# Zero matmuls in TensorE's planned gaps at the start of a two-layer cross-attention and feed-forward kernel

## The chip, the cores and the metric

The kernel runs on one core of a Trainium2 chip. The metric is the device time of one execution in microseconds (us); several runs are summed up by their median. The profile belongs to one profiled execution, and its span reaches from the first to the last instruction on the core.

## The reference, cut to what matters

The input is `x`, 8192 tokens of width 128 in 128 sequences of 64 tokens, and a context of the same shape. Four blocks are added onto `x` one after the other, in float32:

```
x = x + xattn0(layernorm(x), ctx)   # 16 heads of width 8, softmax over 64 keys, gate, layer norms
x = x + ffn0(layernorm(x))          # silu(x w1) * (x w2), gelu(. h1), gelu(. h2), . w3 ; hidden 512
x = x + xattn1(layernorm(x), ctx)   # 16 heads, softmax over 64 keys
x = x + ffn1(layernorm(x))          # relu(x W1 + b1) W2 + b2 ; hidden 512
```

## The kernel before

**Tiling.** The 8192 tokens are cut into 16 chunks of 512 tokens (`NCH`, `CH`). A chunk lies in SBUF as 4 groups of 128 tokens. For each chunk there are four streams of work, which are Python generators: `attention0`, `ffn0`, `attention1` and `ffn1`. Attention handles a chunk in two halves of four sequences (`attend`). The steps of one half are: "scores" on TensorE (line 519), the row maximum on VectorE (line 523), four small VectorE steps that split the maximum into three bf16 parts (532 to 535), "max transpose" on TensorE (538), its copy on ScalarE (541), "scores less max" on TensorE (550), the exponential on ScalarE (555), "weighted values" on TensorE (569), two masked copies on ScalarE (579, 580), the sums and the reciprocal on VectorE (582 to 587), and the product on GpSimd (598). The output projection is "tokens" (`token_major`, line 623). `normalised` holds a layer norm (394 to 421), `transposed` the four transposes (431) and their copy (436 or 438), and `queries`, `keys` and `values` the projections (447, 460, 475). The feed-forward block `ffn0` has "w12" (724, 725), its tanh and products (728 to 732), and the two 512 by 512 layers "h" (764).

**Order.** The program's order on every engine is fixed while the program is being built, by a planner, the class `Order`. Each stream yields `Op`s, one for each stage on one engine. `LENGTHS` gives each name its planned duration and a lag, both in planned us. The planner keeps a clock for each engine. It repeatedly takes the operation that can start earliest in planned time, with priorities between the streams, advances that engine's clock, and lets the generator emit its instructions. An operation on one engine can start after an operation on another by the constant `LAT` (0.08) and that operation's lag. Buffers are planned too: `RESOURCES` counts the slots of each kind, among them the eight PSUM banks ("bank"; scores use banks 0 to 3 together), and a released slot carries the planned time from which it is free. What the chip does is not bound to those times: there each engine runs its own instructions in the planned order, and waits only for data and buffers.

**The start.** Loads are issued from SyncE in the order written in the code. GpSimd first makes constants (the identity, `vblk` of line 328, `nmax` of line 337), and then helps with the layer norms (382, 383). The first TensorE operation is a bias matmul in `constants` (643); after it come the transposes and projections of chunks 0 and 1, then their attention halves (chunk 0, then chunk 1), and then chunk 0's `ffn0`. The streams of chunk 2 wait until the first large layer of chunk 0's `ffn0` is under way (`AHEAD`, `marks`).

**The context for the second attention** is loaded turned (line 291), token by token into columns, into slots of kind "c".

Of the kernel before, what the change touches and what calls it, by code (L numbers as in the profile page):

```python
# [9 lines left out]
BF16 = mybir.dt.bfloat16  # L10
# [4 lines left out]
P = 128  # L15
# [33 lines left out]
}  # L49
TRACE = []  # L50
AHEAD = 2
SWAP = [*range(16, 32), *range(16)]

LAT = 0.08
PE, DVE, ACT, POOL, SP = "PE", "DVE", "ACT", "POOL", "SP"
# [22 lines left out]
class Op:  # L78
# [5 lines left out]
    def __init__(self, engine, name, get=None, put=(), after=None, table=None, prio=None):  # L84
        self.engine, self.name, self.get, self.put = engine, name, get or {}, list(put)
        self.after, self.table, self.prio, self.end = after, table, prio, None
        self.us, self.lag = LENGTHS[name]
# [14 lines left out]
class Order:  # L102
# [4 lines left out]
    def __init__(self, resources):  # L107
        self.clock = dict.fromkeys((PE, DVE, ACT, POOL, SP), 0.0)
        self.free = {k: [(0.0, i) for i in range(n)] for k, n in resources.items()}
        self.table, self.streams, self.waiting, self.log = None, [], [], []  # L110
        self.tiling = 0

    def add(self, gen, prio, deps=()):
# [19 lines left out]
    def choice(self, kind, n, t):  # L133


        if kind == "sc":
            f = [x for x in self.free["bank"] if x[1] < 4]
            return f if len(f) == 4 else None
        f = self.free[kind]
        if kind == "bank":  # L140
            f = sorted(f, key=lambda x: (max(x[0], t), x[1] < 4, x[0]))
        else:
            f = sorted(f)
        return f[:n] if len(f) >= n else None

    def advance(self, s, value=None):
        while True:
            try:
                got = s.gen.send(value)
            except StopIteration:  # L150
                s.done = True
                if s in self.streams:
                    self.streams.remove(s)
                return
            if isinstance(got, tuple):
                value = Stream(got[0], got[1], ())
                value.ends = list(s.ends)
                self.streams.append(value)
                self.advance(value)
            elif isinstance(got, list):  # L160
                s.op, s.deps = None, got
                return
            else:
                s.op = got
                return
# [15 lines left out]
    def run(self):  # L181
        while True:
            self.begin()
            best = None
            for n, s in enumerate(self.streams):
                if s.op is not None:
                    t = self.start_of(s)
                    if t is not None:
                        other = s.op.table not in (None, self.table)
                        prio = s.prio if s.op.prio is None else s.op.prio  # L190
                        key = (t + (0.6 if other else 0.0), prio, n)
                        if best is None or key < best[0]:
                            best = (key, s, t)
            if best is None:
                assert not self.streams and not self.waiting
                return
            _, s, t = best
            op, op.slots = s.op, {}
            for kind, n in op.get.items():
                f = self.choice(kind, n, t)  # L200
                kind_of = "bank" if kind == "sc" else kind
                op.slots[kind] = [(kind_of, i) for _, i in f]
                self.free[kind_of] = [x for x in self.free[kind_of] if x not in f]
            op.end = t + op.us
            if op.engine == PE and TILING.get(op.name, 0) != self.tiling:
                self.tiling = TILING.get(op.name, 0)
                op.end += CHANGE
            if op.table not in (None, self.table):
                self.table = op.table
                op.end += 1.3  # L210
            self.clock[op.engine] = op.end
            for kind, i in op.put:
                self.free[kind].append((op.end + LAT + max(op.lag, 0.0), i))
            self.log.append((op, [op.after] if op.after else s.ends, t))
            s.ends = [op]
            self.advance(s, op)
# [3 lines left out]
def kernel(  # L220
# [16 lines left out]
    nc = tc.nc  # L237
# [4 lines left out]
    const = ctx.enter_context(tc.tile_pool(name="const", bufs=1))  # L242
# [6 lines left out]
    banks = psum.tile([P, 8, DH], F32, tag="banks", name="banks")  # L249
# [23 lines left out]
    def load(name, shape, src):  # L273
        t = const.tile(shape, F32, tag=name, name=name)
        nc.sync.dma_start(t, src)
        return t
# [17 lines left out]
    order = Order(RESOURCES)  # L294
# [12 lines left out]
    wf1 = load("wf1", [P, DH], w_f1)  # L307
    wf2 = load("wf2", [P, 4, D], w_f2)

    ident = const.tile([P, P], F32, tag="ident", name="ident")  # L310
    make_identity(nc, ident)

# [13 lines left out]
    for i in range(N_VB):  # L326
        t = resident.tile([P, 32, 3, 2, 8], F32, tag=f"vblk{i}", name=f"vblk{i}")
# [7 lines left out]
    for i in range(N_NM):  # L335
        t = resident.tile([P, 4, 32], BF16, tag=f"nmax{i}", name=f"nmax{i}")
# [167 lines left out]
    def attend(got, half):  # L504
# [61 lines left out]
        for s in range(HS):  # L566
# [20 lines left out]
        nc.vector.stream_shuffle(  # L587
            rec.rearrange("p s q -> p (s q)"), su.rearrange("p s q -> p (s q)"), SWAP
        )
# [101 lines left out]
    def attention0(ci, prio):  # L691
        got = {"free": []}
        xt = x_sb[ci]
        con = yield (context0(ci, got, prio), prio)
        z, fz = yield from normalised(xt, twice=True)
        if ci == 0:
            consts.append((yield (constants(), prio)))
        yield consts
        gat = yield (gate0(z, got), prio)
        qnT, fq = yield from transposed(z, (), colv("L0_xattn_ln_q_g"), colv("L0_xattn_ln_q_b"))  # L700
        got["qx"], f = yield from queries(wa0[:, 0, :], qnT, bq0, fq)
        got["free"] += f
        yield [con, gat]
        yield Op(DVE, "free", put=fz)
        if ci == 0:
            biases[0] = yield from out_bias(wa0[:, 3, :], "L0_xattn_bv", "L0_xattn_bo", "bo0")
        oT, fo = yield from attention(got, prio)
        po, fp = yield from token_major([(oT, wa0[:, 3, :])], fo)
        op = yield Op(DVE, "from bank", get={"wk": 1}, put=fp)
        o = tile_of(op.slots["wk"][0], (P, NG, D))  # L710
        nc.vector.tensor_tensor(o, po, biases[0], ALU.add)
        y, fy = yield from normalised(o, gate=got["gate"])
        yield Op(POOL, "add 3", put=fy + op.slots["wk"])
        nc.gpsimd.tensor_tensor(y, y, rowv("L0_xattn_ln_o_g"), ALU.mult)
        nc.gpsimd.tensor_tensor(xt, xt, rowv("L0_xattn_ln_o_b"), ALU.add)
        nc.gpsimd.tensor_tensor(xt, xt, y, ALU.add)  # L716
# [127 lines left out]
    for ci in range(NCH):  # L844
        marks.append(Stream(None, 0, ()))
        a0.append(order.add(attention0(ci, 1), 1, a0[-2:-1] + marks[-AHEAD - 1 : -AHEAD]))
        first = ci == NCH - 1
# [56 lines left out]
```

## Time and profile before

| | |
|---|---|
| median of 3 runs | 1228.09 us (1226.3 to 1228.68) |
| time of the profiled execution | 1228.58 us |
| its span | 1226.8 us |
| mean granted TensorE clock over the span | 0.976 |
| busy: PE, PEld | 1158.8 us (94%), 708.0 us (58%) |
| busy: DVE, ACT, POOL | 891.3 us (73%), 578.2 us (47%), 329.9 us (27%) |
| chain that ended last: PE, DVE, ACT | 78%, 16%, 2% |
| PE busy from 14.28 to 96.44 us | 55.09 of 82.16 us, at a mean granted clock of 0.69 |
| PE busy from 96.44 us to the end | 1103.70 of 1130.36 us |

PE is TensorE's matmul side, PEld its weight load, DVE VectorE, ACT ScalarE, POOL GpSimd, SP SyncE. PEclk is the clock that TensorE was granted, as a share of full speed. The chain that ended last is followed back from the last instruction; "issue" in it is time in which nothing that the profile shows was waited for. A line such as `L569` is line 569 of the kernel, `x64` the number of instructions merged, and a float32 matmul of one call shows as two instructions.

### The profile page before, as it was taken

The page shows a single profiled execution, that of the slowest core. Times are in us where ns is not written, and L with a number is a line of the kernel's source. Part 1 is how long each engine was busy: PE and PEld are TensorE (multiplying, and loading weights), DVE is VectorE, ACT ScalarE, POOL GpSimd, SP SyncE. Part 2 cuts the span into 40 slices and gives each one's busy share as a digit, 9 for nine tenths or more (in the row PEclk, how much of TensorE's full clock was granted, in tenths as well). Part 3 has the DMA queues.
Part 4 walks back from the last instruction along what each step waited for, and adds up shares of the span by engine and source line. Part 5 has one row for each costly group of instructions (what it writes and reads, how often), then busy time and mean ns, then how long its engine had stood idle before and what let it go on. Part 6 is the DMA issues. An engine that isn't in the chain of part 4 may idle for free.

```text
span 1226.8 us, 31151 instructions
## 1 busy us (share of the span) xinstructions
PE 1158.8 (94%) x13446; PEld 708.0 (58%) x13446; DVE 891.3 (73%) x2357; ACT 578.2 (47%) x733; POOL 329.9 (27%) x505
## 2 busy tenths in 40 slices
PE   4669999999999999999999999999999999999998
PEld 2544555565655656565655557565565556546676
DVE  5565677697769877777768869766897768822795
ACT  2124555644456454445556374445636564333310
POOL 5041142133214241413214313221423113401310
PEclk9569999999999999999999999999999999999999
DMA  9999994919197990949397891999993000000001
GB/s 213 10 23 24 25 10 20 16 13 9 19 8 30 7 31 2 8 29 9 20 8 22 14 24 11 9 6 16 9 9 11 2 2 2 10 1 1 10 19 43
DMA packets 1075753, 23.11 MB, mean 19 GB/s; under 512 B 1050016, under 2 KB 1074592, under 8 KB 1075488
## 3 DMA queue, kind: packets, MB, share of 16 engines
q1 hardware_dynamic: 1075616, 21.13, 87.4%
q8 instruction: 105, 1.72, 0.8%
q14 instruction: 32, 0.26, 0.1%
HBM read 16.93 MB, written 4.19 MB: 17 GB/s over the span
## 4 chain that ended last, share of the span: by engine, by line
PE 78%; DVE 16%; ACT 2%; issue 1%; POOL 1%; DMA 1%; SPq 0%; DVEq 0%; ACTq 0%
PE banks L764 32%; PE banks L623 10%; PE banks L550 7%; PE banks L569 5%; PE banks L519 4%; PE banks L724 4%; PE banks L810 4%; PE banks L725 4%; DVE m L523 3%; PE banks L475 2%; DVE wk L421 2%; PE banks L431 2%; PE banks L447 2%; PE banks L460 2%; DVE st L394 2%
## 5 line engine op out<-in xcount | busy, mean ns | idle before, releaser
L764 PE MATMUL banks<-hid,wh 128*128 128x512 f32 x1024 | 475.8, 602 | 1.5 <-DVE hid L732 1.3
L764 PEld LDWEIGHTS banks<-hid,wh 128*128 128x128 f32 x1024 | 183.3, 190 | 187.9 <-issue 167.2
L523 DVE TENSOR_REDUCE m<-banks 128x32 f32<-128x2048 f32 x64 | 146.2, 2284 | 30.9 <-PE banks L519 30.7
L598 POOL TENSOR_TENSOR wk<-av,rec 128x256 f32<-128x256 f32 x64 | 46.7, 730 | 452.1 <-DVE rec L587 384.0
L738 ACT ACTIVATE hid<-banks,col 128x512 f32<-128x512 f32 x128 | 87.9, 687 | 167.8 <-PE banks L764 167.3
L555 ACT ACTIVATE e<-banks 128x2048 f32<-128x2048 f32 x64 | 120.1, 1877 | 25.0 <-PE banks L550 24.5
L586 DVE RECIPROCAL su<-su 128x256 f32<-128x256 f32 x64 | 111.5, 1743 | 0.1
L582 DVE SCALAR_TENSOR_TENSOR su<-banks,mask,su 128x256 f32<-128x256 f32 x64 | 30.9, 482 | 103.4 <-ACT av L580 102.8
L383 POOL TENSOR_TENSOR nr<-nv,neg_half 128x4 f32<-128x4 f32 x96 | 97.5, 1015 | 8.0
L738 ACT ACT_TABLE_LOAD x62 | 79.5, 1283 | 29.5 <-PE banks L764 28.6
L519 PEld LDWEIGHTS banks<-kx,qx 32*128 32x128 f32 x2048 | 65.8, 193 | 42.5 <-issue 13.7
L541 ACT COPY nmT<-banks 128x128 bf16<-128x128 bf16 x64 | 16.9, 264 | 154.6 <-PE banks L538 147.8
L569 PEld LDWEIGHTS banks<-e,vblk 128*32 128x32 f32 x4096 | 62.9, 113 | 43.6 <-ACT e L555 29.8
L569 PE MATMUL banks<-e,vblk 128*32 128x64 f32 x4096 | 73.8, 225 | 9.7 <-ACT e L555 7.9
L519 PE MATMUL banks<-kx,qx 32*128 32x128 f32 x2048 | 78.5, 290 | 3.0 <-DVE m L523 2.6
L728 ACT ACTIVATE wk<-banks,half_s 128x512 f32<-128x512 f32 x64 | 43.9, 687 | 74.0 <-PE banks L724 73.2
L550 PE MATMUL banks<-qx,kx 32*128 32x128 f32 x2048 | 75.5, 286 | 0.8 <-issue 0.8
L724 PE MATMUL banks<-wk,w 128*128 128x512 f32 x128 | 68.5, 618 | 2.7 <-DVE wk L438 2.7
L555 ACT ACT_TABLE_LOAD x48 | 61.6, 1283 | 13.9 <-PE banks L550 12.6
L550 PEld LDWEIGHTS banks<-qx,kx 32*128 32x128 f32 x2048 | 66.2, 196 | 1.7 <-issue 1.7
L394 DVE BATCH_NORM_STATS2 st<-x 128x6 f32<-128x128 f32 x256 | 55.3, 278 | 16.0 <-POOL x L716 11.5
L725 PE MATMUL banks<-wk,w 128*128 128x512 f32 x128 | 66.5, 601 | 0.0
(113 smaller groups left out, 1738.7 us busy)
## 6 DMA issues: line engine op xcount, KB each, us to landing
c<-in_c_dram SPq DMA_DIRECT2D x32, 256.0 KB, 41.1
x<-in_x_dram SPq DMA_DIRECT2D x16, 256.0 KB, 3.5
out_dram<-x SPq DMA_DIRECT2D x16, 256.0 KB, 2.3
wh<-in_w_h_dram SPq DMA_DIRECT2D x1, 2048.0 KB, 11.5
wa<-in_w_a_dram SPq DMA_DIRECT2D x2, 256.0 KB, 5.9
w<-in_w_dram SPq DMA_DIRECT2D x1, 512.0 KB, 7.1
wf<-in_w_f_dram SPq DMA_DIRECT2D x2, 256.0 KB, 7.2
row<-in_rows_dram SPq DMA_DIRECT2D x1, 384.0 KB, 5.4
```

Of the source, the lines that this page charges most:

```text
L383: nc.gpsimd.tensor_tensor(rs, ve, neg_half, ALU.pow)
L519: nc.tensor.matmul(sc[:, g, s, :], qs[h, s, :], ks[h, s, :], start=True, stop=True)
L523: nc.vector.tensor_reduce(m, sc.rearrange("p g s (j k) -> p g (s j) k", j=2), AX.X, ALU.max, negate=True,)
L550: nc.tensor.matmul(sT[:, g, s, :], lhs, rhs, start=(n == 0), stop=(n == 1), skip_group_check=True)
L555: nc.scalar.activation(e.rearrange("p g s i q -> p (g s i q)"), sT.rearrange("p g s c -> p (g s c)"), AF.Exp, scale=SCALE,)
L569: nc.tensor.matmul(po[32 * g : 32 * g + 32, i, s, :], vb[:, 4 * (half * HS + s) + g, i : i + 2].rearrange("p h j d -> p (h j d)"), e[:, g, ...
L586: nc.vector.reciprocal(su, su)
L623: nc.tensor.matmul(ps[:, g, :], lhs[:, g * P : (g + 1) * P], w, start=(n == 0), stop=(n == len(blocks) - 1),)
L724: nc.tensor.matmul(pa, w12[:, 0, k * P : (k + 1) * P], zT, start=True, stop=True)
L725: nc.tensor.matmul(pb, w12[:, 1, k * P : (k + 1) * P], zT, start=True, stop=True)
L738: nc.scalar.activation(h, ps, AF.Gelu, scale=scale)
L764: nc.tensor.matmul(ps, wh[:, l, k, o * P : (o + 1) * P], hid[k][0], start=(k == 0), stop=(k == 3))
```

## The change

A bf16 tile `blank` of 128 by 128 is set to zero by GpSimd, ahead of the identity and all other constants. A function `busy(n, bank)` issues `n` matmuls of `blank` with `blank`, each 128 by 128 by 128, into the first 128 columns of a PSUM bank; nobody reads them. Sixty of them go into bank 7 before anything else on TensorE. Beyond that, whenever the planner places a TensorE operation whose planned start is below 95 (`RAMP`), it first calls `fill`: the planned gap before that operation, times 0.8, divided by 0.11 (`FILLER`) and cut to a whole number, is the number of zero matmuls that are issued ahead of it, into the free bank with the highest number that the operation itself does not take. The planner's clocks and slots are not changed by this, so the order of all other work stays what it was.

```
+RAMP, FILLER = 95.0, 0.11
...
         self.table, self.streams, self.waiting, self.log = None, [], [], []
+        self.busy = None
...
+    def fill(self, t, op):
+
+        n = int((t - self.clock[PE]) * 0.8 / FILLER)
+        taken = [i for f in op.slots.values() for kind, i in f if kind == "bank"]
+        free = [x for x in self.free["bank"] if x[1] not in taken and x[0] <= self.clock[PE] + 0.2]
+        if n > 0 and free:
+            self.busy(n, max(free, key=lambda x: x[1])[1])
...
                 self.free[kind_of] = [x for x in self.free[kind_of] if x not in f]
+            if op.engine == PE and t < RAMP:
+                self.fill(t, op)
             op.end = t + op.us
...
     wf2 = load("wf2", [P, 4, D], w_f2)
 
+    blank = const.tile([P, P], BF16, tag="blank", name="blank")
+    nc.gpsimd.memset(blank, 0.0)
+
+    def busy(n, bank):
+        for _ in range(n):
+            nc.tensor.matmul(banks[:, bank, 0:P], blank, blank, start=True, stop=True)
+
+    order.busy = busy
+    busy(60, 7)
     ident = const.tile([P, P], F32, tag="ident", name="ident")
```

## The prediction

> **What bounds the kernel now.** I read the page's 40 slices first. From slice 3 on PE is busy 90% or more and so it is TensorE that sets the time; before that it is not busy, and its clock is not full either.
>
> ```profile
> PE   4669999999999999999999999999999999999998
> PEclk9569999999999999999999999999999999999999
> ```
>
> So slices 0 to 2, some 92 us, are a stage of their own. I then cut it into stretches of 3.41 us, because the points at which the granted clock changes (27.55, 30.96, 34.38, 71.92, 78.75, 88.99 us) all lie on one such grid. The columns are the stretch, its length, busy us of PE, PEld, DVE, ACT and POOL, granted clock, DMA share and GB/s.
>
> ```profile
> 24.14:27.55 3.41, 1.16 (x4) 0.40 (x6) 0.11 (x2) 2.57 (x6) 0.00 (x0) 1.00 1.88 7
> 27.55:30.96 3.41, 3.41 (x50) 3.07 (x54) 2.92 (x8) 0.58 (x1) 0.00 (x0) 0.50 1.89 7
> 30.96:34.38 3.42, 1.00 (x34) 0.81 (x31) 2.70 (x4) 0.00 (x0) 0.00 (x0) 1.00 1.85 12
> 34.38:37.79 3.41, 1.72 (x33) 1.30 (x25) 2.29 (x4) 0.27 (x1) 0.00 (x0) 0.50 1.89 7
> ...
> 51.44:54.85 3.41, 2.67 (x36) 2.15 (x28) 2.93 (x6) 0.41 (x2) 0.00 (x0) 0.50 1.86 11
> ...
> 68.51:71.92 3.41, 3.01 (x74) 2.54 (x64) 1.82 (x3) 1.10 (x3) 0.00 (x0) 0.50 1.84 7
> 71.92:75.33 3.41, 1.74 (x68) 1.46 (x68) 2.19 (x11) 2.19 (x3) 1.74 (x3) 1.00 1.85 12
> 75.33:78.75 3.42, 0.00 (x0) 0.00 (x0) 3.08 (x6) 0.26 (x1) 0.23 (x2) 1.00 1.89 7
> ```
>
> Read the PE column against the clock of the next row. A stretch busy for 3.41 or 3.01 us (88%) is followed by full clock. One of 2.67 us (78%) at half clock is followed by half clock. At full clock, 1.16 and 1.00 us (34%, 29%) and 0.00 lose it, while 1.74 us (51%) keeps it. So the clock is won at some 80 to 88% of a stretch and lost somewhere between 34 and 51%.
>
> The price stands in the chain of waits: the same TensorE groups early and late.
>
> ```profile
> 38.27 2.48 PE banks L550 x37
> 40.76 0.02 issue
> 40.78 1.89 ACT e L555
> 42.66 0.04 issue
> 42.71 1.93 PE banks L569 x64
> 44.64 2.41 PE banks L550 x45
> ...
> 123.80 1.28 PE banks L550 x48
> ...
> 130.12 1.10 PE banks L569 x64
> ```
>
> PE and ACT (or DVE) alternate in this stage: each half waits out the other engine. So PE time saved here is time saved on the chain, though PE is only 67% busy (55.09 of 82.16 us).
>
> **What the Trainium skill says.** "TensorE: Matmul & The Clock Gate", Part 1, says that the array runs at half clock until an activity window has been busy, that the window is 3413 ns long and runs free of the kernel, and that an idle one halves the clock again. This trace agrees, with the 3.41 us grid. The page says that the monitor watches how busy TensorE is; it does not say whether zeros count. Part 2, Back-to-back issue gap, gives about 81 ns for one weight load and one matmul of 128 columns in a stream. No bf16 stream of that shape is in this trace.
>
> **Price of a zero matmul.** Nearest rows: L623 (128x128x128, float32) goes at 2.73 us for 24, 114 ns each at full clock; its weight loads last 192 ns, the bf16 load of L538 96 ns. Half of 114 is 57 ns as the low bound, the bf16 load alone, 96 ns, the high one. I take the page's 81 ns. At half clock I estimate twice that range, 0.11 to 0.19 us.
>
> **How many, and what covers them.** The counts follow from `LENGTHS`. Between "scores" and the next "scores" the planner sees 0.28 (LAT and lag) + 2.3 (max) + 0.08 = 2.66, so int(2.66 x 0.8 / 0.11) = 19. Before "weighted values" it sees 0.28 + 1.9 + 0.08 = 2.26, so 16. Carried through to planned time 95 this gives 316 in the gaps and 60 ahead: 376. In order, with the real idle time that was there:
>
> - Before L643: 60 + 53. PE idles until 14.28. GpSimd's zeros should be there near 1 us. Some 6 us at 0.11 and the rest at 0.081 end by about 12 us. Cover left: 2 us.
> - 6 before L431, 5 before L352, 7 before L519: no real idle time. These 18 lie on the path: 1.5 us. They eat warm-clock savings.
> - 7 (idle 0.87), 16 (2.31), 19 (2.42), 17 (2.18), 14 (1.79), 16 (2.00), 23 (2.42), 14 (1.84), 16 (2.07), 16 before L724 (1.69): each n x 0.081 is 0.57 to 1.86 and fits, even at 0.096 (23 take 2.2).
> - 39 before each L623 group. The first: after "scores" (1.10) they take 3.2, the projection 1.1, together 5.4 of the 7.0 us that DVE needs until L538 at 58.01. The second: 3.2 + 0.5 for two of the four token groups, against 4.77 until POOL's product at 79.46.
> - 9 before the last L764 of the first group: 0.73 against 0.64 idle.
>
> Between 14 and 96 us, 263 fillers take 21 us; with the work at full clock (some 38 us) that is near 59 of 68 us. No stretch should fall below half busy, so the clock should hold once won.
>
> **What the full clock saves,** row by row along the chain, warm price from later rows (L519 1.10, L550 1.28, L569 1.03 to 1.10, L475 1.08, L431 x8 0.86, L460 about 1.10 after idle):
>
> - 14.28 to 26.39: L460 2.08, L431 1.71, then L447. Up to 2.0 less, but POOL and ACT (qx, 2.3 us on the chain) take over, and the clock may have lapsed in the 2 us before 14.28. I take 1.2 (0.5 to 2.0).
> - 26.39 to 31.68: L460 1.12, L475 1.85, L352 0.73, L519 1.58 = 5.28; warm 3.64, plus 12 fillers 0.97. Saved 0.7.
> - 31.68 to 50.99: L519 1.86, L550 2.48, L569 1.93, L550 2.41, L569 1.98 = 10.66; warm 5.80. Saved 4.9. ACT's 1.89 and DVE's 2.30 stay.
> - 50.99 to 58.01: ACT and DVE only. Saved 0.
> - 58.01 to 74.74: 0.29 + 2.07 + 2.48 + 1.94 + 2.42 + 1.15 = 10.35; warm 5.96. Saved 4.4.
> - 74.74 to 83.27: L623 1.24 to about 0.6. Saved 0.6.
> - 83.27 to 96.44: L724 and L725 2.07 + 1.71 + 1.71 + 1.04, warm 1.10 + 3 x 0.86: 2.85. DVE's layer norm (L394, which waits for POOL L716) is queued ahead of the last L730 and may come late next. I take 2.5.
>
> Sum 14.3. Added: the memset on POOL, which is busy without a break from 0.7 to 9 us and feeds L421 at 12.70. The like MEMSET of `ones` reads 0.21 us; I take 0.15. Another 0.1 for the nine. **Net 14.1 us.** After 96.44 PE is busy 1103.70 of 1130.36 us and the rest moves up as it is. The turned loads do not stop this: the first is through by 60.2 us (SP's next issue) and is first read at 140.1. Added instruction fetch has no row to price it; between nothing and 1 us, and I take nothing. The profiled execution took 1228.58, which becomes 1214.5; against the median of 1228.09 that is 1214.0.
>
> **The rivals.**
> - *The clock is held only in part.* One late filler or one emptier stretch costs it, and winning it back takes a whole busy stretch. For: the 2 us hole before 14.28, and planned gaps that are not the real ones. Half of the gain: 7 us, 1221 (1217 to 1225).
> - *Zeros do not count as activity.* Then fillers run at half clock, in order, ahead of work that waits behind them on PE. At 0.11 us they overrun by some 2.5 us (the 18 on the path 1.9, the rest small): 1230.5. At 0.16 us each of the larger groups overruns too: 4.8 at the start, 3.7 and 2.6 at the two of 39, 2.9 for the 18, some 6.4 elsewhere, 20 in all: 1248. It decides once the clock stays at 0.50 through the first 113. Against it: 32-column L569 and zero-filled `vblk` operands stood in the stretch that won the clock at 71.92, so plain busy time seems to count.
> - *Given back later,* if the bulk were set by loads or DVE: no change, 1228. PE's waits name no DMA, so this is slight.
>
> **How the numbers follow.** Clock held 0.70 (1211 to 1217), held in part 0.18, given back 0.04, zeros do not count 0.08. A measurement tells about 0.2%, 2.5 us, from no change. Faster 0.88, same 0.04, slower 0.08. The low end, 1210.5, is all of the 15.9 us of PE savings with the cheapest filler and a little more; the high end, 1221, is the middle of the second case.
>
> **What would show it.** PEclk should read 9 in slices 1 and 2; L550 near 31 us should last 1.28 and L569 1.10; the first L764 group of 20 should start near 82; DVE rows should keep their durations. Filler groups at over 0.11 us, or a clock of 0.50 after 20 us, would make the forecast wrong. So would a longer PE idle time after 90 us.

## The result, and the profile after

| | before | after |
|---|---|---|
| median | 1228.01 us (6 runs, 1226.3 to 1231.7) | 1218.6 us (6 runs, 1215.98 to 1220.41) |
| profiled execution, its span | 1228.58, 1226.8 us | 1220.41, 1218.6 us |
| instructions in the span | 31151 | 31904 |

The ratio is 0.9918, with a 95% interval of 0.9901 to 0.9935: faster by 9.4 us, where 14.1 were forecast. The profiled execution happens to be the slowest of the six; the positions below are its own.

The 40 slices of the page after, PE's busy tenths and its granted clock:

```profile
PE   7779999999999999999999999999999999999998
PEclk8899999999999999999999999999999999999899
```

Slice 2 reads the 9 that was forecast for the clock; slice 1 reads only 8. The stretches of 3.41 us show where the clock is missing; they now lie on a grid of their own (columns as in the prediction).

```profile
3.34:6.76 3.42, 3.42 (x35) 3.42 (x34) 0.64 (x6) 1.28 (x1) 3.21 (x5) 1.00 0.83 232
6.76:10.17 3.41, 3.41 (x61) 3.26 (x58) 2.00 (x16) 0.00 (x0) 3.09 (x14) 1.00 0.92 282
10.17:13.58 3.41, 0.03 (x1) 0.00 (x0) 2.93 (x19) 0.00 (x0) 2.84 (x8) 1.00 1.08 451
13.58:16.99 3.41, 2.56 (x17) 2.47 (x18) 3.27 (x18) 0.26 (x1) 2.92 (x7) 0.50 0.97 342
16.99:20.41 3.42, 3.30 (x12) 1.89 (x10) 2.64 (x13) 0.52 (x1) 2.02 (x4) 0.50 1.07 358
...
44.30:47.71 3.41, 1.52 (x68) 1.24 (x69) 1.59 (x5) 1.73 (x3) 0.73 (x1) 1.00 1.85 11
47.71:51.13 3.42, 2.15 (x30) 1.93 (x30) 2.59 (x6) 0.00 (x0) 0.72 (x1) 0.50 1.88 7
51.13:54.54 3.41, 3.41 (x34) 3.41 (x33) 3.00 (x5) 0.00 (x0) 0.00 (x0) 0.50 1.85 11
54.54:57.95 3.41, 3.41 (x65) 3.13 (x63) 1.92 (x10) 0.27 (x1) 0.00 (x0) 1.00 1.88 7
```

Two things are to be seen. The zeros won the clock: in the first two rows only fillers run, 35 of them and then 61 in the same time (the recorded clock of 1.00 there is not the real one in the first). And the clock is lost twice, after a stretch with 0.03 us of work, and after one with 1.52 us (45%). A later one with 1.65 us (48%, 71.61 to 75.02 us) kept it.

The chain of waits has the groups that the forecast priced, at full clock (lines 550 and 569 of before are 571 and 590 now), and something that it did not have:

```profile
37.09 1.40 PE banks L571 x48
38.49 0.02 issue
38.52 1.89 ACT e L576
40.40 0.04 issue
40.45 1.10 PE banks L590 x64
41.55 0.17 PE banks L571 x4
41.72 0.24 issue
41.96 1.34 PE banks L571 x44
...
46.35 0.42 PE banks L540 x4
46.77 2.21 issue
48.98 2.08 PE banks L540 x24
51.05 3.96 PE banks L327 x39
55.02 0.96 PE banks L644 x8
```

In the middle of the 32 matmuls of one "scores" TensorE stands for 2.21 us and waits for nothing that the profile shows. That hole made the stretch of 1.52 us; the clock was then 0.50, the 39 fillers took 3.96 us, and the projection of L644 behind them was late.

The waits of TensorE between 12 and 92 us (us in total, times, the longest) name three such holes:

```profile
PE banks L540 <- issue: 2.2, 1, 2.2
...
PE banks L590 <- issue: 1.2, 1, 1.2
PE banks L571 <- issue: 0.2, 1, 0.2
```

**Where they fall.** Counting TensorE's matmuls from the start in the timeline, the three holes come after number 478, 606 and 990. Each is 94 plus a multiple of 128. A matmul comes with a weight load, so this is every 256 instructions. The page's instruction queue fits that:

```profile
q8 instruction: 108, 1.77, 0.9%
```

Before it had 105 packets; 753 more instructions came in 3 more, 251 each. So the theory for the missing microseconds was **supply**: TensorE's program arrives in pieces of about 256 instructions by DMA, and a piece is late when the previous one is used up sooner than the next can be fetched beside the turned loads. The rivals were **cover** (the fillers leave too much of a gap idle, and the clock lapses for that) and **banks** (a filler waits for the last reader of its bank).

### The profile page after: what moved, and what is told of

The parts are those of the page before. It is cut to its first block, busy times and chain, and to the rows that moved or that the text cites. A ratio compares the mean times of both kernels' runs of the same rounds, so it can differ in the third digit from the quotient of the medians.

```text
span 1218.6 us, 31904 instructions
## 1 busy us (share of the span) xinstructions
PE 1171.4 (96%) x13822; PEld 723.6 (59%) x13822; DVE 891.2 (73%) x2357; ACT 578.1 (47%) x733; POOL 329.9 (27%) x506
## 2 busy tenths in 40 slices
DMA packets 1075756, 23.16 MB, mean 19 GB/s; under 512 B 1050016, under 2 KB 1074592, under 8 KB 1075488
## 3 DMA queue, kind: packets, MB, share of 16 engines
q8 instruction: 108, 1.77, 0.9%
## 4 chain that ended last, share of the span: by engine, by line
PE 78%; DVE 15%; POOL 2%; ACT 2%; issue 2%; DVEq 0%; ACTq 0%; POOLq 0%
PE banks L785 32%; PE banks L644 10%; PE banks L571 6%; PE banks L590 5%; PE banks L540 4%; PE banks L831 4%; PE banks L745 4%; PE banks L746 4%; DVE m L544 3%; PE banks L496 2%; PE banks L452 2%; DVE wk L442 2%; PE banks L468 2%; PE banks L481 2%; DVE st L415 2%
## 5 line engine op out<-in xcount | busy, mean ns | idle before, releaser
L571 PE MATMUL banks<-qx,kx 32*128 32x128 f32 x2048 | 72.1, 277 | 0.6 <-issue 0.5
L745 PE MATMUL banks<-wk,w 128*128 128x512 f32 x128 | 66.7, 603 | 1.8 <-DVE wk L459 1.8
L746 PE MATMUL banks<-wk,w 128*128 128x512 f32 x128 | 65.4, 592 | 0.0
L644 PE MATMUL banks<-wf,hid 128*128 128x128 f32 x512 | 64.1, 277 | 1.3 <-ACT nmT L562 0.8
```

Of the source, the lines that this page charges most:

```text
L571: nc.tensor.matmul(sT[:, g, s, :], lhs, rhs, start=(n == 0), stop=(n == 1), skip_group_check=True)
L644: nc.tensor.matmul(ps[:, g, :], lhs[:, g * P : (g + 1) * P], w, start=(n == 0), stop=(n == len(blocks) - 1),)
L745: nc.tensor.matmul(pa, w12[:, 0, k * P : (k + 1) * P], zT, start=True, stop=True)
L746: nc.tensor.matmul(pb, w12[:, 1, k * P : (k + 1) * P], zT, start=True, stop=True)
```

## The experiments

**Wide fillers.** A filler of 512 columns does the same TensorE time in a quarter of the instructions.

```
-RAMP, FILLER = 95.0, 0.11
+RAMP, FILLER = 95.0, 0.44
...
-    blank = const.tile([P, P], BF16, tag="blank", name="blank")
+    blank = const.tile([P, DH], BF16, tag="blank", name="blank")
...
-            nc.tensor.matmul(banks[:, bank, 0:P], blank, blank, start=True, stop=True)
+            nc.tensor.matmul(banks[:, bank, :], blank[:, 0:P], blank, start=True, stop=True)
...
-    busy(60, 7)
+    busy(15, 7)
```

> The changed kernel with each filler four times as wide (128 by 512) and a quarter as many, so about the same TensorE time in about a quarter of the added instructions. Theory 'instruction supply': the gaps of 2.21 and 1.17 us that end on 'issue' come when TensorE runs through pieces of its program, 128 load-and-matmul pairs each, faster than they are fetched beside the turned load; with fewer instructions no such gap over 0.5 us is left before 90 us, the clock is not lost at 48 us, the way from the end of the second 'weighted values' to the first 'scores less max' of chunk 1 shrinks from 13.75 to 10.7 to 11.2 us, and the time is 1214 to 1216 us. Rival 'clock only': the clock is lost because fillers leave too much idle time in certain windows; the busy time is the same or a little less here, so it is lost again near 48 us and the time stays at 1218 to 1220. Rival 'banks': a filler waits for the last reader of its bank; nothing changes in that, 1218 to 1219.

Measured: 1219.14 us, ratio 0.9925 (0.9909 to 0.9941). The expectation of supply was missed, and the time is the one that the rivals gave. But the holes did not stay where they were: they last 1.68 and 0.70 us and now stand after number 350 and 734, again 94 plus a multiple of 128. Neither rival gives a reason why holes should keep this distance when instructions are taken out. What fails in the theory of supply is that the fillers are what uses the pieces up. In the timeline, matmuls 222 to 350 began at about 37.5 us and were through at 42.4, nearly all of them attention's own small matmuls at full clock; the next piece was there at 44.1.

**Two straight loads.** A turned load moves its bytes as single float32 numbers: the page of the changed kernel counts 1050016 DMA packets under 512 bytes, and with all sixteen loads straight (below) 1440.

```
+    cs_v = c.rearrange("(c p a) d -> c p (a d)", p=P, a=NG)
...
-        nc.sync.dma_start(ct_sb[ci][0], ct_v[ci])
+        nc.sync.dma_start(ct_sb[ci][0], (cs_v if ci < 2 else ct_v)[ci])
```

> The kernel before, with the context loads of line 291 for chunks 0 and 1 done straight instead of turned (same bytes, contiguous; the second attention of these two chunks then computes on wrongly laid out context). The DMA engines are then nearly free up to 90 us. All theories: the kernel before shows no 'issue' gap over 0.3 us before 90 us, so nothing is won: 1226 to 1229 us.

> The changed kernel with the same two context loads done straight (the same part is computed on wrongly laid out context). Instruction supply: with the DMA engines free the pieces arrive in time, the gaps at 46.8 and 69.0 us vanish, and it gains 3 to 4 us on the changed kernel: 1214 to 1216 us. Clock only, and banks: as the changed kernel, 1218 to 1220 us.

Measured: the base 1226.96 us, ratio 0.9995 (0.9988 to 1.0001); the changed kernel 1217.07 us, ratio 0.9906 (0.9888 to 0.9923). This did not test what it was made for. The third load, still turned, was issued at 23 us, so the DMA share stood at 1.8 to 1.9 from 30 to 63 us, and the hole at number 606 was there with 2.20 us. The hole at number 990, at 66.8 us and so just after that load (DMA share 0.04 from 65 to 70 us), was down from 1.17 to 0.59 us.

**All loads straight.** The same with `cs_v` for every chunk.

> The kernel before with all sixteen context loads of line 291 done straight (contiguous, same bytes; the whole second attention then computes on wrongly laid out context). It is the base for the changed kernel with the same loads. The 'issue' gaps of TensorE that the kernel before shows after 96 us, some 3.6 us in all, should go if they are program pieces fetched late beside the turned loads: 1224 to 1227 us. If those gaps have nothing to do with the loads: 1226 to 1229 us.

> The changed kernel with all sixteen context loads done straight (the same wrong layout). Two straight loads only let the third, turned one start at 23 us, so the DMA engines stayed full and the gaps stayed; here they are free from some 30 us on. Theory 'program pieces fetched late beside the turned load': no 'issue' gap over 0.3 us before 90 us, the clock stays full from 21 us on, 4 us or more below the changed kernel: 1212 to 1215 us, and some 12 us below its own base. Rival 'a piece takes 6 to 7 us to fetch whatever the loads do': the gaps stay near 2.2 and 1.2 us and the time stays at 1217 to 1219 us.

Measured: the base 1220.28 us, ratio 0.9938 (0.9923 to 0.9953), which is lower than either theory gave; the changed kernel 1211.05 us, ratio 0.9861 (0.9843 to 0.988), also just below what supply gave. In both, one wait of TensorE on "issue" is left after the first matmul, a short one at L644 (L623 before) that all kernels have; for the changed one:

```profile
PE banks L644 <- issue: 0.3, 1, 0.3
```

So the holes are tied to the turned loads: without those none is left, in either kernel, with the fillers as they were. The start of the first large group of the 512 by 512 layer moves from 88.86 to 84.58 us in the changed kernel and from 96.44 to 96.16 in the base. The medians say less. The turned loads cost the kernel before 7.5 us as well (1227.76 in the same rounds; in the profiled executions 6.9 us of it lie after that group), and the gap between changed kernel and base is 9.2 us where it was 9.4 and some 12 were expected. In the stage itself the holes cost the profiled execution some 4 us; by how much they hurt an average execution of the changed kernel more than one of the kernel before, the medians do not resolve. The clock, which was to stay full from 21 us on, still lapsed near 53 and 71 us.

**The pieces themselves.** The trace keeps the start and the length of every DMA packet, those of the instruction queue too; each of these (`q8`) has 16384 bytes. Their number fits TensorE's program alone: its 13822 matmuls and as many weight loads, 27644 together, are 108 pieces of 256. In the changed kernel the packets end shortly before the holes do:

| hole after number | TensorE goes on at | last packet before | time from its end |
|---|---|---|---|
| 478 | 41.96 us | 37.84 to 39.96 us | 2.0 us |
| 606 | 48.98 us | 45.10 to 47.30 us | 1.7 us |
| 990 | 70.21 us | 66.49 to 68.02 us | 2.2 us |

In all kernels together there are 78 holes of over 0.15 us, the short one at L644 (L623 before) left out, and in every one TensorE goes on 1.4 to 2.3 us after the end of such a packet; the times that lie so after a packet are some 8% of the span. Between 20 and 60 us a packet takes 2.13 to 2.19 us in the changed kernel, and 1.00 to 1.28 us with all loads straight. So the holes are waits for the program, and the turned loads slow its transfer.

**Only the start.** `RAMP` 8.0: the 113 fillers ahead of the first matmul and no others.

> Only the 113 fillers before the first bias matmul, none in the later gaps. They end at 10.2 us and the clock lapses before work comes at 14.4 us, so both theories expect nothing of them: the clock goes as in the kernel before from 20 us on, 1226 to 1229 us. If the fillers at the start were worth something by themselves, the time would be 1224 us or less.

Measured: 1227.39 us, ratio 1.0 (0.999 to 1.0009). They are worth nothing alone; the granted clock is 0.50 again from 15 to 20 us.

**A longer start.** As with wide fillers, but `busy(33, 7)`: 46 fillers that end at 13.5 us.

> As the kernel with wide fillers, but 33 instead of 15 of them before everything else, which adds some 3.9 us of filler at full clock and reaches from 10.2 to about 14 us. If the lapse of the clock in the hole of 4.2 us before the first bias matmul cost what the forecast counted on, the first projection lasts 1.1 instead of 2.07 us, the second projection of the keys starts near 25.5 instead of 26.7, and the time is 1.0 to 1.4 us below the kernel with 15. Rival: that stage is set by POOL and ACT, and nothing changes (within 0.4 us).

Measured: 1216.22 us, ratio 0.9898 (0.9879 to 0.9918), 2.9 us below the kernel with 15, though the two intervals overlap. In the profile the first L481 lasts 1.13 us and the second starts at 25.50 instead of 26.81. That is the 1.3 us that were expected. They are not sure to come: of the four profiles with this start three show 1.12 or 1.13 us for this L481, and one, full cover below, 2.08. The rest goes with where the pieces end: one hole of 1.69 us, again at 94 plus a multiple of 128, and no lapse of the clock until about 70 us.

**A later turned load.** The same, and the first turned load is held back by a memset of one column of its tile on GpSimd, which is planned behind chunk 0's first attention (`a0[0]`).

```
+        if ci == 0:
+            nc.gpsimd.memset(ct_sb[0][0][:, 0:1], 0.0)
         nc.sync.dma_start(ct_sb[ci][0], ct_v[ci])
...
+            if ci == 3:
+                yield [a0[0]]
             op = yield Op(SP, "load turned", get={"c": 1})
```

> As the kernel with 46 wide fillers ahead of the first bias matmul, and the first turned load held back until GpSimd has finished chunk 0's first attention (near 62 us), by a one-column memset of its tile on GpSimd; the order on all engines stays the same. Program pieces fetched late beside the turned load: no 'issue' gap over 0.3 us before 60 us, the first large L785 group starts at 81 to 82.5 us instead of 83.6, and the time is 1213 to 1215 us. Rival 'a piece takes 6 to 7 us to fetch whatever the loads do': as the kernel with 46 wide fillers, 1216 us. If the turned loads, some 45 us later, then come late for the second attention (first needed near 127 us), the time rises above 1220 us.

Measured: 1216.68 us, ratio 0.9911 (0.9895 to 0.9926). No hole is left before 125 us, as supply has it, but nothing is won: the large group starts at 84.57 us, where it started at 83.57 without the hold. TensorE is idle from 50.0 to 51.6 us and again from 68.3 to 70.6, ahead of L561 and the second part of L646, and the clock is at 0.50 afterwards. Without the hole the cover is what fails; what supply expected of the time was missed.

**The real price.** One number, `FILLER` 0.056, so that a group covers 0.8 of a planned gap; with turned and with straight loads.

> The changed kernel with one number changed: FILLER 0.056 instead of 0.11, the time that a filler was measured to take at full clock, so that the fillers cover 0.8 of a planned gap where they covered 0.41. About twice as many fillers, 165 of them at the start, which end near 13 us. Theory 'cover': the clock is lost where a filler group leaves too much of a gap idle; it stays full from 14.4 us on unless a program piece comes late, and the time is 1213 to 1216 us. Rival 'supply': more instructions use the pieces up sooner, the 'issue' gaps before 90 us add to over 3.6 us, and the time is 1218 us or more. The fillers that no idle time covers double as well, about 0.7 us, counted in both.

> The same with all sixteen context loads done straight (the second attention then computes on wrongly laid out context), which took away every late program piece. Cover: with 1211.05 us for the changed kernel in this state, whose clock lapsed at 14, near 53 and near 71 us, full clock there saves 2.5 to 5 us more: 1206 to 1208.5 us, and a granted clock of 1.00 in every stretch of 5 us from 15 to 90 us. Rival 'supply only': the late pieces were the whole loss, so nothing more is to be won: 1210.5 to 1212 us.

Measured with turned loads: 1228.63 us, ratio 1.0012 (1.0003 to 1.0021). The gain is gone, though the granted clock is 1.00 in all stretches of 5 us from 20 us on but the one at 75. The waits between 12 and 92 us:

```profile
PE banks L590 <- issue: 4.7, 2, 2.8
PE banks L327 <- issue: 4.2, 2, 2.8
PE banks L664 <- DVE gw L661: 2.7, 1, 2.7
PE banks L571 <- issue: 0.9, 1, 0.9
```

Five holes, 9.8 us, where the changed kernel has 3.6. Here more fillers do use the pieces up: 632 more instructions, and what the stage gained at full clock is paid back in waits for the program: the large group starts at 96.72 us, against 96.44 in the kernel before.

With straight loads: 1210.42 us, ratio 0.9864 (0.9846 to 0.9882), against 1211.05. No hole, full clock from 20 us on, and still less gain than cover had expected. The groups that no idle time covers doubled with the rest: 11 and 15 at the start, the first of them at half clock, put the first L481 at 18.46 instead of 17.56; the 10, 14 and 19 that follow take 0.6, 0.8 and 1.1 us at 56 ns. What full clock won near 53 and 71 us, they gave back: the large group starts at 84.69 us, against 84.58.

**Full cover with wide fillers.** `FILLER` 0.22, `busy(20, 7)` and with it again 46 wide fillers at the start, none in planned gaps under 1.4; the second kernel also with the later turned load.

```
-        if n > 0 and free:
+        if n > 0 and free and t - self.clock[PE] > 1.4:
```

> Turned loads as in the kernel before, wide fillers (128 by 512) at 0.22 us each, so that they cover 0.8 of a planned gap in about the instructions of the changed kernel's half; 46 of them ahead of the first bias matmul; none in planned gaps under 1.4 us, which had no real idle time. Cover: clock full from 14.7 us on but for late pieces, 1212.5 to 1215 us, below the 1216.2 us of the kernel with 0.44 for a wide filler. Supply: late pieces decide, 1215.5 to 1217 us.

> The same and the first turned load held back to near 62 us by the one-column memset. With the smaller fillers this hold alone won nothing, because the clock lapsed at 51 us instead. Cover: now no 'issue' gap and no lapse before 60 us, 1211 to 1213.5 us, the fastest of the kernels that compute the reference. Rival: the later load only moves the late pieces to where TensorE has no slack, 1214 to 1217 us.

Measured: 1218.97 us, ratio 0.9937 (0.9922 to 0.9952), and with the later load 1217.2 us, ratio 0.9921 (0.9904 to 0.9938). Both miss. In the profile of the first the clock lapsed at the start and at a hole of 1.68 us. The second is the stage as the forecast had imagined it, at full clock from beginning to end:

```profile
14.00:20.00 6.00, 4.25 (x26) 2.50 (x28) 5.07 (x26) 1.75 (x3) 4.86 (x10) 1.00 1.03 341
20.00:40.00 20.00, 17.97 (x284) 10.44 (x280) 13.66 (x40) 7.87 (x13) 0.00 (x0) 1.00 0.09 24
40.00:60.00 20.00, 18.45 (x356) 11.59 (x351) 14.57 (x33) 5.86 (x8) 5.76 (x9) 1.00 0.01 3
60.00:83.00 23.00, 21.58 (x186) 11.00 (x182) 18.61 (x53) 7.59 (x10) 10.78 (x16) 1.00 1.35 8
```

Its large group starts at 82.89 us, 13.55 earlier than before. But its span ends at 1214.7, and so 1.4 us of that are lost in the 1130 us that follow, where one hole, at 891 us, lasts 1.77. The late load is not its cause: the kernel without it has the same hole, at 892 us, with 2.05 us. Of the kernels that compute the reference, the lowest median is that of the longer start, 1216.22 us; its interval overlaps with the changed kernel's, so it is not shown to be better.

## Why the prediction was right, and what it missed

The prediction had the mechanism right, and its range took in the measured 1218.6 us through its upper end, which came from the rival "held only in part". The case that it held most likely, 1211 to 1217, did not come, and the point of 1214.0 was 4.6 us too low. The stage, by starts of the same TensorE work in the profiled executions; a minus is time saved against the kernel before (for the straight pair, against its own base).

| from, to | forecast | after | all straight | full cover, late load |
|---|---|---|---|---|
| start of the first bias matmul | +0.15 | +0.15 | +0.15 | +0.47 |
| to keys of chunk 1 (L460) | -1.2 | +0.15 | 0.0 | -1.32 |
| to the end of chunk 0's second L569 | -5.6 | -4.89 | -4.71 | -5.59 |
| to chunk 1's first L550 | -1.1 | +1.95 | -0.77 | -0.77 |
| to the end of chunk 1's second L569 | -3.3 | -1.57 | -3.56 | -3.01 |
| to L724 | -0.6 | -0.54 | -0.17 | -0.50 |
| to the last L764 of the first group | -2.4 | -2.83 | -2.52 | -2.83 |
| sum | -14.05 | -7.58 | -11.58 | -13.55 |

- **What bounds the kernel: right.** Time saved on TensorE ahead of the large group moved the whole rest up: after it the profiled execution takes 1129.7 us where it took 1130.4.
- **That zeros win and hold the clock: right,** and shown by the first 113, which go at 107 ns and then at 56. The limits read from the profile of before hold: 45% of a stretch, which lies between the 34 and 51% given there, loses the clock.
- **The price of a filler: mis-sized.** 56 ns at full clock, at the low bound of 57, and not the 81 of the Trainium skill. The page "TensorE: Matmul & The Clock Gate" gives both figures; it is what it calls the isolated gap, about 56 ns for 128 columns (Part 2, Back-to-back issue gap), that agrees, though each filler here comes with its weight load. A cheaper filler looked harmless. It is what failed at the start: "end by about 12 us. Cover left: 2 us" became 10.2 us and a hole of 4.2 us, and a whole stretch lay in it. The 1.2 us of that row did not come; the longer start brought them in three of its four profiles.
- **"No stretch should fall below half busy": failed,** for two reasons. In the changed kernel a late piece of program emptied the stretch at 44.3 us. Where no piece was late, idle times that fillers of 56 ns do not cover did it, with straight loads near 53 and 71 us.
- **"Added instruction fetch ... between nothing and 1 us, and I take nothing": the largest miss.** In the rows to L550 and to the second L569 of chunk 1 the holes of 2.21 and 1.17 us, and the half clock after the first, go with 2.7 and 2.0 us against the pair without turned loads; over all rows it is 4.0 (-7.58 against -11.58). This is of the profiled executions; the medians, 9.4 and 9.2 us, do not show it. It is not only the added instructions: attention itself gets through 128 matmuls in some 5 us at full clock. And the term had a row. The kernel before waits on "issue" too, 3.6 us in all, and its chain shows it soon after the stage:

```profile
136.28 0.69 PE banks L569 x38
136.96 0.72 issue
137.68 0.65 PE banks L569 x26
```

This one comes after number 1116, two short of 94 plus eight times 128. What stands ahead of the prediction, that an engine waits only for data and buffers, leaves this out.
- **ACT and DVE keep their durations: right** (1.89 and 2.30 us in both chains). The row to L724, in which they decide, gave 0.54 of 0.6.
- **The rivals.** "Held only in part" is what happened, at 1221 in the forecast and 1218.6 measured; "zeros do not count" and "given back later" did not. The forecast of 1214.0 was of the stage at full clock; the kernel that has it gained 13.55 us there, and its median is 1217.2.

## What to carry to other kernels

Work that only keeps TensorE's clock has to be sized by its measured time at full clock, laid over real idle time rather than planned idle time, and given out in few, wide instructions. Here this filled the stage, but no kernel made so had a median below that of the changed kernel by more than the noise. At full clock the next limit can be the program itself: where DMA engines are full of small descriptors, a chain of small matmuls waits for its own instructions, and each filler added is an instruction more to fetch. Count the instructions between waits on "issue"; equal distances give that limit away, and the packets of the instruction queue, where a trace has them, confirm it.

## What the runs showed of the hardware

- TensorE's waits on "issue" in this stage come at distances that are multiples of 128 matmuls with their weight loads, in six kernels; packets in the instruction queue grow by one for each 251 added instructions in the changed kernel (277 with 0.056). Later in the kernel the position drifts slowly: in the kernel before it is 2 short of 94 plus a multiple of 128 at 137 us, and 34 short at 906 us, 79 pieces in. That would fit other instructions in the stream or missing records; it was not followed up.
- Beside a turned load (DMA share 1.8 to 1.9) the pieces followed each other every 7.0 to 7.3 us: their packets start at 30.77, 37.84, 45.10 and 52.14 us in the changed kernel, and at 39.42, 46.73 and 54.01 us with 0.056. With all loads straight and 0.056 they start as close together as 3.8 us in the stage (42.30 and 46.05 us), and no hole is left. Why a packet starts when it does was not looked into.
- The granted clock as recorded cannot be trusted before its first change: 1.00 is shown while fillers go at 107 ns, and in the kernel before while L460 lasts 2.08 us.
- Two kernels with the same TensorE work up to 20 us (full cover, with and without the later load) differ at the start: the first L481 lasts 2.08 us in one and 1.12 in the other. The Trainium skill, "TensorE: Matmul & The Clock Gate", Part 1, has the window run free of the kernel, so where a stretch begins is chance; the two profiles agree with that and do not prove it.
